# Softmax denominators of an attention layer: when they are summed, and in groups of how many heads

## The chip, the cores and the metric

The kernel runs on one core of a Trainium2 chip. Its engines work at the same time and wait for each other by semaphores: TensorE (PE in the profile) multiplies matrices, VectorE (DVE) adds and multiplies tiles, ScalarE (ACT) evaluates functions and copies, GpSimd (POOL) does elementwise work and issues DMAs, SyncE (SP) issues DMAs. The metric is the device time of one execution in microseconds (us), the median of several.

## The reference

The input x has 4 images (batches) of 1024 channels and 32 x 32 places, so 1024 tokens each. All is float32. Layer 0 is attention with 16 heads of 64, layer 1 a bottleneck of convolutions with batch norms.

```python
x = hidden_states.reshape(B, C, N).transpose(0, 2, 1); residual = x
qkv = (x @ w_qkv.T + b_qkv).reshape(B, N, 3, nh, hd)
q, k = rmsnorm(rope(q)), rmsnorm(rope(k))            # norm over all heads of a token
attn = softmax(einsum('bqhd,bkhd->bhqk', q, k) * hd ** -0.5)
ctx = einsum('bhqk,bkhd->bqhd', attn, v)
x = rmsnorm(ctx @ w_proj.T) + residual               # layer 0
y = relu(bn(conv1x1(x))); y = relu(bn(conv3x3(y))); y = bn(conv1x1(y))
out = relu(x + softplus(residual_scale) * y)         # layer 1
```

The kernel leaves the bias of v out of v and adds it to the context, since the weights of a softmax sum to one.

## The kernel before

The batches run one after the other. Each has four projections (q, k, v, and y after the attention) and the attention itself. The projections of all batches but parts of the first use two nested levels of a scheme that needs seven block products instead of eight; each of its 49 quarter products is four matmuls of 256 columns. The weights' sums for it are prepared once, for a large part on DVE during the attention of batch 0 ("made", lines L397 to L400 and L414 to L417), written back to memory by POOL (L402, L419) and loaded from there by SP (L388, L411) into a ring of eight slots.

Attention of a batch goes over two halves of the queries (`c`, 512 queries each) and in each over eight head pairs (`hp`). A pair has eight steps `t`, one for each 128 keys: PE computes the scores of both heads (L786) into one of three score banks (`sc`, two PSUM banks each), ACT takes the exponential (L793) into `p`, and DVE adds `p` to the pair's denominators (L804, L806: 128 keys x 2 heads x 512 queries). Then PE multiplies the exponentials with v (L815); ACT copies the context (L821). The context comes in two parts. In batch 0 the second is copied by ACT (L824) and added by a DMA of POOL (L825), in the others DVE adds it (L850).

What is left of a denominator is a sum over the 128 partitions, and PE does it, with a matrix of ones. Two pairs, so four heads, form a group (`sums_of_four`, L868: four matmuls of 128x32 into one bank `dn`). The step is kept in the list `late` and runs in the next pair after step 1; for the last group of a batch it runs at once at the end of the attention (`last_inverses`). In the first half of the queries of batches 1 to 3 the denominators are first folded: DMAs of POOL (`halve`, L878 to L881) add the lower and the upper 64 partitions, so that one group of four matmuls (`sum_of_eight`, L887) serves eight heads. It runs at the end of the second pair after its last one.

After a group the reciprocals follow. ACT copies `dn` out (L915, L889, L928), SP writes it to memory and reads it back with few values a partition (L903, L907), DVE takes the reciprocal (L919, L894), SP writes it (L920, L895) and reads it broadcast over the partitions (L937). This second part, `invert`, lies in the list `half_done`; one entry is taken at the end of a pair. The tiles so loaded go to the list `ready`, and at the end of every second pair `mean_of_v` multiplies the contexts by them on DVE (L769) and adds the bias of v on POOL (L770). For the last group the reciprocal is taken of the whole tile (L929), with POOL's DMAs, and the products come in the projection.

Order: PE, POOL, DVE and ACT execute in the order in which the program text issues (`manual_schedule`); only SP's instructions are ordered by the framework. In the projections steps can be put off with `after(n, step)`, n in units of four matmuls of 512 columns or eight of 256 (about 3.43 us); `product_done` runs those that are due. In the attention, weight preparation (`extra`) is spread over the pairs by a count of `slots`, and `load_parts` loads at step 3 so that at most two sets are held.

PSUM is divided anew for each stage:

```python
"proj": [("o1", [P, CH], 4), ("o2", [P, CH], 4)],
"att": [("sc", [P, 2, CH], 3), ("cx", [P, 2, CH], 1)],
```

Of the kernel before, what the change touches and what calls it, by code (L numbers as in the profile page):

```python
# [18 lines left out]
P = 128  # L19
# [66 lines left out]
def program(ctx, tc, x, wblk, w2, w3, vecs, cos, sin, out, bad):  # L86
# [76 lines left out]
    with tc.tile_pool(name=f"st{u}", bufs=2) as st, ExitStack() as s:  # L163
# [95 lines left out]
        def after(n, step):  # L259
            later.append((pace["at"] + n, step))  # L260
# [505 lines left out]
        def mean_of_v(q_all, c, hp, w, engine=nc.gpsimd):  # L766

            cx = q_all[:, hp, half[c]]
            nc.vector.tensor_tensor(cx, cx, w, ALU.mult)  # L769
            engine.tensor_scalar(cx, cx, col("bv", hp), None, ALU.add)  # L770

        def attention(b, c, q_all, k_all, v, probs_, late, ready, extra, slow, steps_in_all, load_parts, fold, then):


            at = half[c]
            sums_, contexts = [], []
            for hp in range(NHP):
                n = f"{b}_{c}_{hp}"
                rows = shifts(q_all, k_all, n, hp, c) if bad is None else None
                probs = []  # L780
                for t in range(N // P):
                    p = probs_[:, t]
                    sc = bank("sc", f"sc_{n}_{t}")
                    for keys in (low, high):
                        for j, d in enumerate((low, high)):
                            nc.tensor.matmul(  # L786
                                sc[keys, j], k_all[d, hp, t * P + keys.start : t * P + keys.stop], q_all[d, hp, at],
                                start=True, stop=bad is not None,
                            )
                    if bad is None:  # L790
                        for j in range(2):
                            nc.tensor.matmul(sc[:, j], ones[0:1, :], rows[j], start=False, stop=True)
                    nc.scalar.activation(p, sc, AF.Exp)  # L793
                    if t == 1:
                        if late:
                            late.pop(0)()
                        if fold and hp % 2 == 0:
                            d_ = fold[hp // 4][:, hp % 4 // 2 * 2 : hp % 4 // 2 * 2 + 2, :]
                        else:
                            d_ = acc.tile([P, 2, CH], F32, tag="tot", name=f"den_{n}")  # L800
                    if t == 3:
                        load_parts()
                    if t == 1:
                        nc.vector.tensor_tensor(d_, probs[0], p, ALU.add)  # L804
                    elif t > 1:
                        nc.vector.tensor_tensor(d_, d_, p, ALU.add)  # L806
                    probs.append(p)
                if (c, hp) == (NCH - 1, NHP - 1):
                    then()
                o = bank("cx", f"cx_{n}")  # L810
                for t in range(N // P):
                    for j in range(2):
                        h0 = (2 * hp + j) * HD
                        for i, keys in enumerate((low, high)):
                            nc.tensor.matmul(  # L815
                                o[j * HD : (j + 1) * HD, i], v[keys, t, h0 : h0 + HD], probs[t][keys, j],
                                start=(t == 0), stop=(t == N // P - 1),
                            )
# [30 lines left out]
                if contexts:  # L849
                    nc.vector.tensor_tensor(contexts[0][0], *contexts.pop(0), ALU.add)  # L850
                if eights and eights[0][0] <= c * NHP + hp:
                    eights.pop(0)[1]()
                if hp % 2 == 0 or fold:
                    continue
                if (c, hp) == (NCH - 1, NHP - 1):
                    last_inverses(b, c, hp, n, sums_of_four(n, sums_), ready)
                else:
                    late.append(lambda n=n, hp=hp, ds=sums_: inverses(b, c, hp, n, sums_of_four(n, ds), ready))
                sums_ = []

        def sums_of_four(n, sums_):
            if n == f"0_{NCH - 1}_{NHP - 1}":
                bank("sc", f"skip_{n}")
            dn = bank("sc", f"dn_{n}")[:, 0]
            for i, d_ in enumerate(sums_):
                for j in range(2):
                    q = slice((2 * i + j) * QH, (2 * i + j + 1) * QH)
                    nc.tensor.matmul(dn[q, :], ones[:, :QH], d_[:, j], start=True, stop=True)  # L868
            return dn

        half_done, eights = [], []
        low, high = slice(0, P // 2), slice(P // 2, P)

        def halve(hp, d_, home):
# [5 lines left out]
                nc.gpsimd.dma_start(home[high], d_[high])  # L880
                nc.gpsimd.dma_start(home[high], d_[low], accum_op=ALU.add)  # L881

        def sum_of_eight(b, n, hp, home, ready):

            dn = bank("sc", f"dn_{n}")[:, 0]
            for i in range(4):
                nc.tensor.matmul(dn[i * QH : (i + 1) * QH, :], halves, home[:, i, :], start=True, stop=True)  # L887
            r = temp(f"rec_{n}")
            nc.scalar.copy(r, dn)  # L889
            k = 2 * b * NCH * NHP + 2 * (hp - 3)  # L890
            few, rows = to_few(n, k, 8, r[:: QH // 2, :])

            def invert():
                nc.vector.reciprocal(few, few)  # L894
                nc.sync.dma_start(rows, few)  # L895
                for i in range(2):
                    at = k + 4 * i
                    spread(0, hp - 2 + 2 * i, n + f"_{i}", ready, [dens[at : at + 2, :], dens[at + 2 : at + 4, :]])
# [11 lines left out]
        def inverses(b, c, hp, n, dn, ready):  # L910


            r = temp(f"rec_{n}")
            k = 2 * ((b * NCH + c) * NHP + hp - 1)
            nc.scalar.copy(r, dn)  # L915
            few, rows = to_few(n, k, 4, r[::QH, :])

            def invert():
                nc.vector.reciprocal(few, few)  # L919
                nc.sync.dma_start(rows, few)  # L920
                spread(c, hp, n, ready, [dens[k + j : k + j + 3 : 2, :] for j in range(2)])
# [293 lines left out]
        for b in range(B):  # L1215
# [60 lines left out]
            slow = [lambda: None] * 3 + [lambda f=f: add_residual(f) for f in range(NT)] if b > 0 else []  # L1276
            probs_ = xp.tile([P, N // P, 2, CH], F32, tag="x", name=f"p_{b}")
            fold = [None, None]
            if b > 0:
# [10 lines left out]
            for c in range(NCH):  # L1290
                if (b, c) == (B - 1, NCH - 1):
                    extra = filters()
                attention(
                    b, c, q_all, k_all, v, probs_, late, ready, extra, slow, steps_in_all, load_parts, fold[c], then
                )
            psum_for("proj")
            room = v_room(f"to_{b}")
# [419 lines left out]
```

## Time and profile before

| what | us |
|---|---|
| median of 3 runs (lowest, highest) | 2649.51 (2647.75, 2649.77) |
| the profiled execution | 2648.69 |
| its span in the profile | 2646.9 |
| PE busy | 2627.9 (99%) |
| DVE busy | 2140.0 (81%) |
| ACT busy | 1122.9 (42%) |
| POOL busy | 470.8 (18%) |
| dn groups of four heads (L868), of eight (L887) | 20 and 6, 8 matmul records each |

The profile shows one execution. A line of its groups gives the program's line, the engine, the operation, out<-in with shapes, the count, then busy time and mean ns, then idle time before and what ended it. A float32 matmul appears as two records. A line of the timeline gives start, length, engine, line and count, and in brackets the engine's idle time before it. A line of the chain gives start, length, what. A line of the waits gives who waited for whom: us in total, times, the longest.

### The profile page before, as it was taken

What the parts mean: (1) busy time and instruction counts of PE and PEld (TensorE: products, weight loads), DVE (VectorE), ACT (ScalarE), POOL (GpSimd) and SP (SyncE); (2) the same over time, 40 slices, a digit from 0 to 9 for tenths busy, and PEclk for the clock granted to TensorE, in tenths of its full rate; (3) what the DMA queues carried; (4) which work ended last, traced back from release to release, by engine and by line L of the source; (5) the groups of instructions that cost most, each with busy time, mean ns of one, the idle gap of its engine ahead of it and who ended that gap; (6) DMA issues with size and microseconds to landing.
All of it is one profiled execution on the core that took longest, in us unless ns stands there. A gap on an engine that the chain in (4) does not pass through costs nothing.

```text
span 2646.9 us, 40534 instructions
## 1 busy us (share of the span) xinstructions
PE 2627.9 (99%) x15452; PEld 1629.4 (62%) x15452; DVE 2140.0 (81%) x2566; ACT 1122.9 (42%) x1576; POOL 470.8 (18%) x592
## 2 busy tenths in 40 slices
PE   9999999999999999999999999999999999999997
PEld 4448433488888333688886333888884335846843
DVE  5567899998887977887878767987988779877977
ACT  2222566523442655433343655233425654312266
POOL 2542244301101221100111222000111221010000
PEclk9999999999999999999999999999999999999999
DMA  8887788777667452456665541665774442683165
GB/s 286 290 255 203 219 253 243 239 224 238 183 182 213 83 103 50 132 179 223 191 191 155 97 85 27 215 206 176 193 213 90 84 105 82 206 279 104 64 235 211
DMA packets 252938, 463.66 MB, mean 175 GB/s; under 512 B 32192, under 2 KB 125168, under 8 KB 252736
## 3 DMA queue, kind: packets, MB, share of 16 engines
q1 hardware_dynamic: 196816, 287.80, 34.3%
q0 software_dynamic: 47856, 156.40, 23.8%
q10 hardware_dynamic: 8064, 16.78, 1.8%
q8 instruction: 125, 2.05, 0.3%
q14 instruction: 77, 0.63, 0.1%
HBM read 329.53 MB, written 97.01 MB: 161 GB/s over the span
## 4 chain that ended last, share of the span: by engine, by line
PE 67%; DVE 1%; ACT 0%; DMA 0%; issue 0%; ACTq 0%
PE sc L786 13%; PE cx L815 12%; PE p_y L490 10%; PE p_v L485 8%; PE p_q L490 6%; PE p_k L490 6%; PE c L1618 3%; PE c2x L1478 2%; PE c2y L1478 2%; PE c L1020 2%; PE c L979 1%; PE c1s L1020 1%; PE dn L868 0%; PE c1a L1020 0%; DMA cosT<-in_cos_dram 0%; ACT h L1602 0%
## 5 line engine op out<-in xcount | busy, mean ns | idle before, releaser
L793 ACT ACTIVATE p<-sc 128x1024 f32<-128x1024 f32 x512 | 478.2, 1049 | 17.7 <-PE sc L786 17.5
L786 PE MATMUL sc<-q,k 64*64 64x512 f32 x4096 | 456.7, 591 | 0.1
L806 DVE TENSOR_TENSOR den<-den,p 128x1024 f32<-128x1024 f32 x312 | 385.5, 1236 | 37.6 <-ACT p L793 5.1
L815 PE MATMUL cx<-p,to 64*64 64x512 f32 x3072 | 338.2, 589 | 0.0
L786 PEld LDWEIGHTS sc<-q,k 64*64 64x64 f32 x4096 | 149.2, 132 | 294.8 <-ACT p L793 151.4
L815 PEld LDWEIGHTS cx<-p,to 64*64 64x64 f32 x3072 | 117.5, 133 | 212.1 <-issue 210.7
L485 PE MATMUL p_v<-w_v,x 128*128 128x256 f32 x928 | 210.0, 379 | 0.8 <-DVE x L456 0.7
L490 PE MATMUL p_y<-q,w_y 128*128 128x256 f32 x928 | 209.8, 379 | 0.7 <-issue 0.7
L490 PEld LDWEIGHTS p_y<-q,w_y 128*128 128x128 f32 x928 | 176.0, 190 | 27.9 <-issue 4.1
L485 PEld LDWEIGHTS p_v<-w_v,x 128*128 128x128 f32 x928 | 176.1, 190 | 26.1 <-DVE x L456 1.3
L821 ACT COPY q<-cx 128x512 f32<-128x512 f32 x64 | 37.5, 585 | 348.0 <-PE cx L815 348.0
L770 POOL TENSOR_SCALAR q<-q,vec 128x512 f32<-128x512 f32 x56 | 108.7, 1966 | 290.3 <-DVE q L769 290.3
L490 PE MATMUL p_q<-to,w_q 128*128 128x256 f32 x672 | 152.2, 379 | 0.0
L490 PE MATMUL p_k<-to,w_k 128*128 128x256 f32 x672 | 152.2, 379 | 0.0
L490 PEld LDWEIGHTS p_k<-to,w_k 128*128 128x128 f32 x672 | 127.4, 190 | 18.4 <-issue 1.2
L490 PEld LDWEIGHTS p_q<-to,w_q 128*128 128x128 f32 x672 | 127.4, 190 | 18.4 <-issue 1.2
L815 PE MATMUL cx<-p,rq 64*64 64x512 f32 x1024 | 112.7, 589 | 0.0
L1618 PE MATMUL c<-h,w 128*128 128x512 f32 x256 | 110.3, 592 | 0.5 <-ACT h L1520 0.5
L804 DVE TENSOR_TENSOR den<-p 128x1024 f32<-128x1024 f32 x52 | 63.5, 1222 | 42.6 <-ACT p L793 42.6
L806 DVE TENSOR_TENSOR den_T<-den_T,p 128x1024 f32<-128x1024 f32 x72 | 88.2, 1225 | 7.5
L485 PE MATMUL p_v<-w_v,t 128*128 128x256 f32 x384 | 90.1, 379 | 0.0
L490 PE MATMUL p_y<-to,w_y 128*128 128x256 f32 x384 | 90.1, 379 | 0.0
(505 smaller groups left out, 4308.5 us busy)
## 6 DMA issues: line engine op xcount, KB each, us to landing
w_v<-wd2f SPq DMA_DIRECT2D x112, 256.0 KB, 3.0
w_y<-wd2f SPq DMA_DIRECT2D x112, 256.0 KB, 3.0
w_q<-wd2f SPq DMA_DIRECT2D x84, 256.0 KB, 2.7
w_k<-wd2f SPq DMA_DIRECT2D x84, 256.0 KB, 2.8
wd2f<-w_pre POOLq DMA_DIRECT2D x68, 256.0 KB, 4.5
q<-qs POOLq DMA_DIRECT2D x64, 256.0 KB, 5.4
k<-ks POOLq DMA_DIRECT2D x64, 256.0 KB, 4.6
x1df<-y POOLq DMA_DIRECT2D x32, 512.0 KB, 5.5
```

The costliest lines, as they stand in the source:

```text
L485: nc.tensor.matmul(o[:, q].rearrange("p (g f) -> p g f", g=2), r[:, i, q * P : (q + 1) * P], wt[:, :, i, :], skip_group_check=True, **at,)
L490: nc.tensor.matmul(o[:, q], wt[:, q, i, :], r[:, i, :], skip_group_check=True, **at)
L770: engine.tensor_scalar(cx, cx, col("bv", hp), None, ALU.add)
L786: nc.tensor.matmul(sc[keys, j], k_all[d, hp, t * P + keys.start : t * P + keys.stop], q_all[d, hp, at], start=True, stop=bad is not None,)
L793: nc.scalar.activation(p, sc, AF.Exp)
L804: nc.vector.tensor_tensor(d_, probs[0], p, ALU.add)
L806: nc.vector.tensor_tensor(d_, d_, p, ALU.add)
L815: nc.tensor.matmul(o[j * HD : (j + 1) * HD, i], v[keys, t, h0 : h0 + HD], probs[t][keys, j], start=(t == 0), stop=(t == N // P - 1),)
L821: nc.scalar.copy(cx, o[:, 0])
L1020: nc.tensor.matmul(o, wt[:, i, :], rows(i), start=first and i == 0, stop=last and i == NH - 1, skip_group_check=True,)
L1478: nc.tensor.matmul(o[:, r * TR * TC : (r + 1) * TR * TC], uw[2 * h + r, j][:, i * PL + f * P : i * PL + (f + 1) * P], vt[b, i][:, 2 * h + ...
L1618: nc.tensor.matmul(os[i], w3t[k][f // NH][:, f % NH, :], h2[b, k][:, half[c]], start=(k == 0), stop=(k == NPT - 1),)
```

## The change

In batch 0 the denominators get a place of their own: two tiles (`own`) used in turn by the groups, instead of the two of the pool `acc`. The sum over partitions runs after step 3 of the next pair instead of step 1 (in the last but one pair still after step 1). `invert` runs after step 2 of the following pair rather than at the end of the pair before it, with exceptions near the end. Batch 0's multiplications by the reciprocals come at the end of even pairs, and the bias of v is added by ACT (`mean_and_bias`, after steps 5 and 6) instead of POOL; in the very last pair by DVE.

In batches 1 and 2 the first four pairs of the second half of queries are folded too, into the tile of the first half's first group. Their group of eight runs one pair after its last pair (in the first half still two pairs after), and its products come at the pair before the last.

The last group of batches 0, 1 and 2 runs half a product into the projection of y, into a bank of the pool `o2`. Weight preparation is spread over 14 instead of 15 pairs.

```diff
-        def attention(b, c, q_all, k_all, v, probs_, late, ready, extra, slow, steps_in_all, load_parts, fold, then):
+        def attention(b, c, q_all, k_all, v, probs_, late, ready, extra, slow, steps_in_all, load_parts, fold, then, own):
...
+            fold_two = 0 < b < B - 1
+            homes = fold
             for hp in range(NHP):
+                fold = homes if homes and hp // 4 < len(homes) else None
...
                     nc.scalar.activation(p, sc, AF.Exp)
+                    if t == (3 if b == 0 and (c, hp) != (NCH - 1, NHP - 2) else 1) and late:
+                        late.pop(0)()
+                    if t in (5, 6) and biases:
+                        biases.pop(0)()
+                    if b == 0 and t == 2 and half_done and half_done[0][0] < c * NHP + hp:
+                        half_done.pop(0)[1]()
                     if t == 1:
-                        if late:
-                            late.pop(0)()
-                        if fold and hp % 2 == 0:
+                        if b == 0:
+                            d_ = own[hp % 4 // 2][:, hp % 2 * 2 : hp % 2 * 2 + 2, :]
+                        elif fold and hp % 2 == 0:
...
-                sums_.append(d_)
-                if hp % 2 == 1:
+                if contexts and b == 0:
+                    add_context(*contexts.pop(0))
+                if not fold:
+                    sums_.append(d_)
+                if hp % 2 == min(b, 1) or c == NCH - 1 and (hp == NHP - 1 or fold_two and hp == NHP - 2):
                     for r in ready:
-                        mean_of_v(q_all, *r)
+                        if b > 0:
+                            mean_of_v(q_all, *r)
+                        elif (c, hp) == (NCH - 1, NHP - 1):
+                            mean_of_v(q_all, *r, nc.vector)
+                        else:
+                            mean_and_bias(q_all, *r)
                     ready.clear()
                 if fold:
                     halve(hp, d_, fold[hp // 4][:, hp % 4 // 2 * 2 : hp % 4 // 2 * 2 + 2, :])
                     if hp % 4 == 3:
-                        eights.append((hp + 2, lambda n=n, hp=hp: sum_of_eight(b, n, hp, fold[hp // 4], ready)))
+                        home = fold[hp // 4]
+                        eights.append(
+                            (c * NHP + hp + 2 - c, lambda n=n, hp=hp, home=home: sum_of_eight(b, c, n, hp, home, ready))
+                        )
...
-                slots = NCH * NHP - 1
+                slots = NCH * NHP - 2
...
                 if (c, hp) == (NCH - 1, NHP - 1):
-                    last_inverses(b, c, hp, n, sums_of_four(n, sums_), ready)
+
+                    def last(ds=sums_):
+                        last_inverses(b, c, hp, n, sums_of_four(n, ds), ready)
+
+                    if b + 1 < B:
+                        after(0.5, last)
+                    else:
+                        last()
...
         def sums_of_four(n, sums_):
-            if n == f"0_{NCH - 1}_{NHP - 1}":
-                bank("sc", f"skip_{n}")
-            dn = bank("sc", f"dn_{n}")[:, 0]
+            dn = bank("o2", f"dn_{n}") if "o2" in psum else bank("sc", f"dn_{n}")[:, 0]
...
+        def add_context(cx, other):
+            nc.vector.tensor_tensor(cx, cx, other, ALU.add)
+
+        def mean_and_bias(q_all, c, hp, w):
+            cx = q_all[:, hp, half[c]]
+            nc.vector.tensor_tensor(cx, cx, w, ALU.mult)
+            biases.append(lambda: nc.scalar.activation(cx, cx, AF.Identity, bias=col("bv", hp)))
...
-            half_done.append((hp + 3, invert))
+            half_done.append((c * NHP + hp + 3 - c, invert))
...
-            half_done.append((0, invert))
+            half_done.append((c * NHP + hp + (1.5 if hp < NHP - 3 or c < NCH - 1 else 1) if b == 0 else 0, invert))
...
+            if b == 0:
+                own = [tp.tile([P, NH, CH], F32, tag=t, name=f"den_{b}_{t}") for t in ("T0", "T2")]
             if b > 0:
 
-                fold[0] = [tp.tile([P, NH, CH], F32, tag=t, name=f"den_{b}_{t}") for t in ("T0", "T2")]
+                fold[0] = homes = [tp.tile([P, NH, CH], F32, tag=t, name=f"den_{b}_{t}") for t in ("T0", "T2")]
+                fold[1] = homes[:1] if b + 1 < B else None
```

More of the change, by code (lines that the diff above doesn't have):

```diff
@@ L848, in attention @@
                     extra.pop(0)()
-                if contexts:
-                    nc.vector.tensor_tensor(contexts[0][0], *contexts.pop(0), ALU.add)
+                if contexts and b > 0:
+                    add_context(*contexts.pop(0))
                 if eights and eights[0][0] <= c * NHP + hp:
@@ L869, in sums_of_four @@
             return dn
-        half_done, eights = [], []
+        half_done, eights, biases = [], [], []
+        def add_context(cx, other):
[4 more added lines that the diff above has]
+            biases.append(lambda: nc.scalar.activation(cx, cx, AF.Identity, bias=col("bv", hp)))
         low, high = slice(0, P // 2), slice(P // 2, P)
@@ L881, in halve, with sum_of_eight @@
                 nc.gpsimd.dma_start(home[high], d_[low], accum_op=ALU.add)
-        def sum_of_eight(b, n, hp, home, ready):
+        def sum_of_eight(b, c, n, hp, home, ready):
             dn = bank("sc", f"dn_{n}")[:, 0]
@@ L889, in sum_of_eight @@
             nc.scalar.copy(r, dn)
-            k = 2 * b * NCH * NHP + 2 * (hp - 3)
+            k = 2 * ((b * NCH + c) * NHP + hp - 3)
             few, rows = to_few(n, k, 8, r[:: QH // 2, :])
@@ L897, in invert @@
                     at = k + 4 * i
-                    spread(0, hp - 2 + 2 * i, n + f"_{i}", ready, [dens[at : at + 2, :], dens[at + 2 : at + 4, :]])
-            half_done.append((hp + 3, invert))
+                    spread(c, hp - 2 + 2 * i, n + f"_{i}", ready, [dens[at : at + 2, :], dens[at + 2 : at + 4, :]])
+            half_done.append((c * NHP + hp + 3 - c, invert))
         def to_few(n, k, rows_, r):
@@ L1278, in program @@
             fold = [None, None]
+            own = None
+            if b == 0:
+                own = [tp.tile([P, NH, CH], F32, tag=t, name=f"den_{b}_{t}") for t in ("T0", "T2")]
             if b > 0:
-                fold[0] = [tp.tile([P, NH, CH], F32, tag=t, name=f"den_{b}_{t}") for t in ("T0", "T2")]
+                fold[0] = homes = [tp.tile([P, NH, CH], F32, tag=t, name=f"den_{b}_{t}") for t in ("T0", "T2")]
+                fold[1] = homes[:1] if b + 1 < B else None
             tc_, two = [], []
@@ L1293, in program @@
                 attention(
-                    b, c, q_all, k_all, v, probs_, late, ready, extra, slow, steps_in_all, load_parts, fold[c], then
+                    b, c, q_all, k_all, v, probs_, late, ready, extra, slow, steps_in_all, load_parts, fold[c], then, own
                 )
```

## Prediction

> **What bounds the kernel now.** I read the busy line first, then the waits of TensorE, then its timeline around the softmax denominators.
>
> ```profile
> PE 2627.9 (99%) x15452; PEld 1629.4 (62%) x15452; DVE 2140.0 (81%) x2566; ACT 1122.9 (42%) x1576; POOL 470.8 (18%) x592
> PE dn L868 <- DVE den L806: 0.9, 1, 0.9
> PE p_y L490 <- issue: 0.7, 1, 0.7
> ```
>
> TensorE (PE) is busy for 2627.9 of 2646.9 us. So only two things can be won: PE instructions that disappear, and the few places where PE stands. The two waits shown are both at the end of batch 0's attention. A third place is no wait in the list; it shows as a stretched group in PE's timeline of batch 0:
>
> ```profile
> 343.77 1.07 PE L868 MATMUL dn<-den,ones 128*32 128x512 f32 x8
> ...
> 372.41 2.21 PE L868 MATMUL dn<-den,ones 128*32 128x512 f32 x8
> ...
> 508.03 7.05 PE L815 MATMUL cx<-p,rq 64*64 64x512 f32 x64
> 515.00 1.05 PE L868 MATMUL dn<-den,ones 128*32 128x512 f32 x4
> 516.98 1.05 PE L868 MATMUL dn<-den,ones 128*32 128x512 f32 x4 [0.92 <-DVE den L806]
> 518.76 3.69 PE L490 MATMUL p_y<-q,w_y 128*128 128x256 f32 x16 [0.73 <-issue]
> ```
>
> The dn group at 372.41 takes 2.21 us where the one before takes 1.07: half of it runs, then it waits. The last group waits for VectorE (DVE), and the first projection matmul starts when ScalarE (ACT) has copied dn (518.08 to 518.66). DVE's timeline says why: it has no gap before those two points, and its last additions end late.
>
> ```profile
> 365.64 7.87 DVE L806 TENSOR_TENSOR den<-den,p 128x1024 f32<-128x1024 f32 x6
> ...
> 402.54 1.60 DVE L400 TENSOR_TENSOR w_pre<-w_pre,w_pre 128x512 f32<-128x512 f32 x1
> ...
> 509.05 7.87 DVE L806 TENSOR_TENSOR den<-den,p 128x1024 f32<-128x1024 f32 x6
> ```
>
> They end at 373.4 and 516.8, after PE asked at 372.4 and 515. In batches 1 and 2 nothing waits; there only the number of dn groups counts. The chain of waits gives the price of one, of four heads inside a head pair and of eight between two:
>
> ```profile
> 1511.10 1.00 PE dn L887 x8
> 1512.10 7.03 PE sc L786 x64
> ...
> 1596.97 1.72 PE sc L786 x16
> 1598.69 1.00 PE dn L868 x8
> 1599.68 5.31 PE sc L786 x48
> ```
>
> Scores of a pair alone take 6.87 us. 1.72 + 1.00 + 5.31 = 8.03 and 1.00 + 7.03 = 8.03, so either kind of group costs 1.16 us: 1.00 of its own and 0.16 around it.
>
> **What the Trainium skill says.** "TensorEngine Tiling (Array Packing)", Key Properties: a change of tiling mode drains the array. The dn tiles are 128x32 between 64x64 ones; the 0.16 us agrees. "GPSIMD Engine Reference", Specifications: GpSimd (POOL) shares its SBUF interfaces with VectorE and they contend when a VectorE instruction has two SBUF inputs. The trace agrees: the 1.60 us above, 0.69 for its neighbours, lies under POOL's bias additions (402.6 to 406.1). "ScalarE: Activation LUTs", Table sets: identity is in every set. So a bias by Identity between exponentials should load no table; the trace shows copies between exponentials without a load, but no Identity there. "DMA: Bandwidth & Descriptors", Anatomy of one DMA: about 2.0 us fixed plus bytes/436e3, an estimate of 2.6 us for 256 KB; the trace has 2.9 for the copy of a fold and 3.5 for its accumulation, and I use these.
>
> **The change, part by part.**
>
> 1. *Batch 0, later groups.* dn moves from step 1 to step 3 of the next pair's eight, 2 x 0.86 = 1.72 us later. The group at 372.4 waited until 373.4, so its 1.14 us (2.21 − 1.07) go. The group itself keeps its 1.16. Score banks: at step 3 dn takes the bank of step 1, whose exponential (0.93 us pitch, from 1.2 us after the pair's start) ends at about 3.1 us, and PE comes at 3.44. No new wait.
>
> 2. *Batch 0's biases* leave POOL (L770, 14 there, 1.97 us mean over the kernel). Twelve go to ACT as Identity, price by the same shape:
>
> ```profile
> L636 ACT ACTIVATE k<-k,vec 128x512 f32<-128x512 f32 x48 | 34.5, 719 | 2.6 <-DVE k L530 2.6
> ```
>
> Two of 0.72 us in every second pair, after the exponentials of steps 5 and 6: the last exponential then ends at 1.2 + 8 x 0.93 + 1.4 = 10.1 us, and PE needs it at 6.87 + 6.0 = 12.9. Hidden, with 2.8 us spare. Two go to DVE (0.49 each). DVE gains what contention cost: the excess over 0.69 of the stretched additions between 346 and 492 sums to about 5.5 us.
>
> 3. *Weight preparation* on DVE is spread over 14 pairs instead of 15: 21 sets of 2.73 us, so 3.0 instead of 2.8 in two pairs, and none is left after pair 6 of the second half. In the profile two sets (502.2 to 507.7) stand ahead of the last pair's additions. Without them these follow the exponentials and end some 10 us after that pair's start, so before PE is done with it (13.7). Per two pairs DVE then has 2 x 9.1 additions + 8.2 preparation + 1.4 reciprocal and multiplications = 27.8 us, against PE's 2 x 13.73 + 1.16 = 28.6. Its cover is 0.8 us per two pairs.
>
> 4. *The reciprocals of batch 0* move from the pair's end to step 2 of the next one. On DVE this is 0.16 us. On SP the write-back, its landing (2.0) and two broadcasts come some 6 us later, and the weight loads queued behind them with them. Those loads wait for free slots anyway (53.4 us of SP's waits in this batch are on written-back weights), and POOL writes them back about 3.5 us sooner without its biases. I price it at 0; bounds −0.5 to +1.5 us of PE time.
>
> 5. *Last group of batches 0 to 2* goes inside the projections, after the first product. Batch 0: from the end of the last pair (514.90) to the first product are 3.86 us; what stays is a group of 1.0 + 0.1. Gain 2.76 us. Batches 1 and 2: 1.06 us before, 1.1 expected after: 0, bounds −0.1 to +0.2 together. The long reciprocal (3.34) and what follows come 0.7 us later; of the sums behind it, those that PE needs first (L287) end at 1674.6 in batch 2 and PE reads them at 1677.7, so 3.1 us cover it.
>
> 6. *Batches 1 and 2, second half:* two groups of four become one of eight: 2 x 1.16 = 2.32 us less on PE. POOL gets six fold DMAs per batch, SP one round trip fewer.
>
> 7. *A new wait.* This group of eight runs one pair after its last head pair; in the first half it is two. POOL does four biases ahead of the last fold. The same sequence stands in the first half of batch 2, for the pair that ended at 1539.7:
>
> ```profile
> 1538.87 8.03 POOL L770 TENSOR_SCALAR q<-q,vec 128x512 f32<-128x512 f32 x4 [12.54 <-DVE q L769]
> 1546.86 0.58 POOL L880 DMA_DIRECT2D den_T<-den  x1
> 1550.09 0.83 POOL L881 DMA_DIRECT2D den_T<-den  x1 [2.66 <-DMA den_T<-den]
> ```
>
> 1550.09 + 3.5 to 3.8 = 1553.6 to 1553.9, 13.9 to 14.2 us after the pair's end. PE asks after 13.73, and behind dn stands the whole next pair. Half of dn's operands are older, which hides up to 0.5; in the second half the biases took 8.36. I take +0.6 us per batch, 1.2 in all; bounds 0 and 2.0.
>
> **Sum:** −1.14 − 2.76 − 2.32 + 1.2 + 0.2 (small delays of parts 4 and 5) = −4.8 us. The profiled execution took 2648.69 us (span 2646.9 and 1.8 around it): 2643.9. It lies 0.8 below the median of the runs shown, 2649.51, so this is 5.6 us (0.21%) below the median. A measurement of this kernel can tell about 0.2%, 5.3 us, from no change; the forecast is just past that.
>
> **Rivals.** *B, the gain is eaten.* The fold arrives late at its upper bound (+2.0 instead of 1.2) and batch 0 still waits for DVE: the first half's third set of weights is asked for a pair earlier, and SP stands there for 28.6 us on slots, so dn at step 3 can wait again, 1 to 2 us. Then 2 to 3 us remain, 2646. For it: DVE's cover is 0.8 us. Against: the waits of DVE on DMA in this batch sum to only 4.9 us now.
>
> *C, slower: DVE becomes batch 0's bound.* Each late load stalls DVE before its additions; what exceeds the cover of 0.8 us per two pairs accumulates over seven groups, and dn waits. To lose 5.3 us in spite of a gain of 4.8, 10.1 us must come up: 0.8 + 10.1/7 = 2.2 us of DMA wait per two pairs, against 4.9/7 = 0.7 now. At 3 us it would be 7 x 2.2 = 15.4 less 4.8: 2659. For it: part 4 delays loads, and the later DVE is, the later SP. Against: slots, not SP, set the loads.
>
> *D, tables:* if Identity were not in the set of the exponential, two biases with an exponential between them would bring four loads (1.28 us each in the trace), 5.1 us, 2.3 over part 2's spare, six times: +14 us. The page excludes it; I leave it 0.01.
>
> **How the numbers follow.** Forecast 0.58, at 2642 to 2644.2; B 0.30, 2644.2 to 2648; C and D 0.12, above 2654.8. The low end takes parts 1, 5, 6 whole, no new wait, and 1 us of spread: 2648.7 − 6.2 − 1 = 2641.5. The high end holds B and the beginning of C: 2651.
>
> **What would show it.** In the profile after: no stretched dn in batch 0 and none waiting for den; projections start within 0.2 us of the last pair; 16 groups of four heads and 8 of eight, where 20 and 6 were before; Identity activations of 0.7 us among batch 0's exponentials without table loads; no POOL bias there. Part 7 is wrong if dn of the second half does not wait for the accumulation. A DVE in batch 0 that waits more than 2 us per two pairs on weights, with dn behind it, would make the whole prediction wrong.

## The result, and the profile after

The changed kernel takes 2646.06 us (median of 22 runs, 2645.12 to 2648.66), the kernel before in the same job 2649.47 (22 runs, 2647.66 to 2652.57). The ratio is 0.9987, with a 95% interval from 0.9982 to 0.9993: a gain of 3.4 us, 0.13%, which lies within the 0.2% that the prediction called no change. The point was 2643.9, 2.2 us too low. The range from 2641.5 to 2651.0 holds the result, the interval called likeliest, 2642 to 2644.2, does not: the range is right because it was wide enough for rival B. By its size the result is rival B, "the gain is eaten" (2646). What ate it is only in part what B named.

The profiled execution took 2645.64 us, its span is 2643.8 (before 2648.69 and 2646.9). In the changed program L893 is the group of four heads (L868 before), L921 the group of eight (L887), L815 the additions to the denominators (L806), L824 the context (L815), L899 the addition of the context's two parts (L850). The busy line and TensorE's waits on what the attention or the projections give, the p_v and p_y lines of the changed kernel:

```profile
PE 2624.5 (99%) x15436; PEld 1628.9 (62%) x15436; DVE 2136.3 (81%) x2566; ACT 1128.4 (43%) x1586; POOL 451.9 (17%) x590
...
PE p_v L485 <- DVE x L456: 1.5, 2, 0.9
...
PE p_y L490 <- issue: 0.8, 2, 0.4
```

PE has 16 records fewer: two dn groups of eight records each. The two waits of before at the end of batch 0 are gone. In their place there are two of p_y at the ends of batches 1 and 2, and p_v waits twice where it waited once. PE's timeline of the changed kernel in batch 0, at the second and third group and at the end:

```profile
345.18 1.07 PE L893 MATMUL dn<-den_T,ones 128*32 128x512 f32 x8
...
373.81 1.07 PE L893 MATMUL dn<-den_T,ones 128*32 128x512 f32 x8
...
506.57 7.05 PE L824 MATMUL cx<-p,rq 64*64 64x512 f32 x64
513.55 1.99 PE L490 MATMUL p_y<-q,w_y 128*128 128x256 f32 x8
515.47 1.06 PE L893 MATMUL dn<-den_T,ones 128*32 128x512 f32 x8
516.47 1.99 PE L490 MATMUL p_y<-q,w_y 128*128 128x256 f32 x8
```

No group is stretched, and the projection starts at 513.55, when the context ends. The same view of the changed kernel at the group of eight in the second half of batch 1, and at the end of that batch:

```profile
1037.89 1.86 PE L921 MATMUL dn<-den_T,halves 128*32 128x512 f32 x8
...
1084.12 1.06 PE L893 MATMUL dn<-den,ones 128*32 128x512 f32 x8
1085.59 1.97 PE L490 MATMUL p_y<-q,w_y 128*128 128x256 f32 x8 [0.41 <-issue]
```

The group of eight takes 1.86 instead of 1.06: it waits 0.80 in its middle. Then the second product of the projection (the next eight p_y records) waits 0.41. In batch 2 it is 1.35 for the group (0.29) and 0.40 for the product.

A ledger of all stages comes from two marks in each batch in PE's timeline: the first matmul of the scores, and the first p_y matmul with y as its input, which follows the second product of the projection. The table gives how much longer (+) or shorter (−) each stretch is than in the profile of the kernel before, in us. Each column is one execution; the forecast's +0.2 for small delays stands in no row.

| stretch | predicted | after | e1 | e2 | e9 | e3 | e4 | e5 |
|---|---|---|---|---|---|---|---|---|
| attention of batch 0 | −3.9 | −4.05 | −3.60 | −2.69 | −3.22 | −1.99 | −2.59 | −3.36 |
| projections, to batch 1 | 0 | +0.16 | +0.24 | +0.58 | +0.05 | −0.02 | −0.08 | −0.08 |
| attention of batch 1 | −0.56 | +0.28 | 0.00 | +0.18 | +0.54 | −0.52 | −0.34 | −0.96 |
| projections, to batch 2 | 0 | +0.88 | −0.05 | +0.84 | +0.94 | +0.47 | +0.75 | +0.15 |
| attention of batch 2 | −0.56 | −0.23 | 0.00 | −0.12 | +0.21 | −0.50 | −0.68 | −0.95 |
| projections, to batch 3 | 0 | +0.35 | 0.00 | +0.43 | −0.01 | +0.21 | +0.53 | −0.01 |
| attention of batch 3 | 0 | −0.52 | −0.15 | −0.52 | −0.50 | −0.51 | −0.51 | −0.50 |

The attention of batch 3 is not changed. Most of its −0.5 belongs to the profile of before: DVE stands for 0.46 us there between two of its own additions (at 2205.49), and the last group of batch 3 is stretched to 1.49 us, against 1.14 in the changed kernel. In e1 DVE stands 0.46 in the same stretch of batch 3, the group takes 1.50, and the gain is missing.

### The profile page after: what moved, and what is told of

The parts are those of the page before. It is cut to its first block, busy times and chain, and to the rows that moved or that the text cites. A ratio compares the mean times of both kernels' runs of the same rounds, so it can differ in the third digit from the quotient of the medians.

```text
span 2643.8 us, 40486 instructions
## 1 busy us (share of the span) xinstructions
PE 2624.5 (99%) x15436; PEld 1628.9 (62%) x15436; DVE 2136.3 (81%) x2566; ACT 1128.4 (43%) x1586; POOL 451.9 (17%) x590
## 5 line engine op out<-in xcount | busy, mean ns | idle before, releaser
L824 PE MATMUL cx<-p,to 64*64 64x512 f32 x3072 | 338.2, 589 | 0.0
L815 DVE TENSOR_TENSOR den<-den,p 128x1024 f32<-128x1024 f32 x192 | 237.9, 1239 | 21.9 <-ACT p L796 2.2
L815 DVE TENSOR_TENSOR den_T<-den_T,p 128x1024 f32<-128x1024 f32 x192 | 236.3, 1231 | 20.4 <-DVE den_T L815 1.4
L824 PEld LDWEIGHTS cx<-p,to 64*64 64x64 f32 x3072 | 117.5, 133 | 212.1 <-issue 211.0
L770 POOL TENSOR_SCALAR q<-q,vec 128x512 f32<-128x512 f32 x42 | 80.5, 1926 | 215.6 <-DVE q L769 215.6
L824 PE MATMUL cx<-p,rq 64*64 64x512 f32 x1024 | 112.7, 589 | 0.0
L732 POOL DMA_DIRECT2D k<-ks x64 | 57.6, 1087 | 180.2 <-ACT p L796 71.3
```

The source lines that it names most:

```text
L732: nc.gpsimd.dma_start(dst[i::2, f, :], other[1 - i :: 2, :], accum_op=ALU.add)
L824: nc.tensor.matmul(o[j * HD : (j + 1) * HD, i], v[keys, t, h0 : h0 + HD], probs[t][keys, j], start=(t == 0), stop=(t == N // P - 1),)
```

## Experiments

Four kernels (e1, e2, e5, e9) share one chip and 47 runs of the kernel before (2649.86), four more (e3, e4, e6, e7) another (23 runs, 2649.51), and the last four (e8, e10, e12, e13) a third (41 runs, 2648.65). Each is compared with the kernel before of its own job. The diffs are against the changed kernel.

**e1: batch 0 alone.** No second fold, and the last group goes into the projection in batch 0 only.

```diff
-            fold_two = 0 < b < B - 1
+            fold_two = False
-                    if b + 1 < B:
+                    if b == 0:
                         after(0.5, last)
-                fold[1] = homes[:1] if b + 1 < B else None
```

> The kernel after with batches 1 and 2 as before (no second fold, their last group at the end of the attention); batch 0 as changed. Theory: the whole gain is batch 0's (4.0 us up to the second product of its y projection), and batches 1 and 2 gave nothing, so this kernel is as fast as the kernel after within 0.5 us: 2645.5, ratio to before 0.9985. Rival, the forecast's own sum: batches 1 and 2 are worth 1.1 us, so this is 1 us slower than after, 2647. On the table waits in the v projections (0.85, 0.67 and a stretch of 0.35 after, one of 0.68 before): if the change in batches 1 and 2 makes them, batches 2 and 3 show none here; if they are scatter or come from batch 0, they show.

Measured: 2647.19, ratio 0.9990 (0.9982 to 0.9998), 2.7 us less. The whole measurable gain is batch 0's. The ledger shows nothing in the stages of batches 1 and 2.

**e9: no second fold**, the last groups still in the projections.

```diff
-            fold_two = 0 < b < B - 1
+            fold_two = False
-                fold[1] = homes[:1] if b + 1 < B else None
```

> The kernel after without the second fold of batches 1 and 2: four groups of four in their second half, the last one still inside the projection. Theory: two groups more cost 2.32 us, the two waits of dn for the fold (1.09) are gone: 1.2 us slower than after, 2647.3, and batches 1 and 2 are then slower than before by their second products' waits. Rival: the fold's DMAs cost PE more than their wait (banks, slower DMAs elsewhere), then this is as fast as after.

Measured: 2647.47, 0.9990 (0.9981 to 0.9998). Against e1 it adds only the last groups of batches 1 and 2, and these stages get 0.54 and 0.21 longer. So moving the group in is not free: 0.31 of batch 1 is a wait of the second product, and about 0.2 in each batch goes without a wait (from the last matmul of the context to the first product with y it takes 5.27 us in batch 2, where it took 5.07 before).

**e2: the last groups of batches 1 and 2 stay at the end**, with the second fold.

```diff
-                    if b + 1 < B:
+                    if b == 0:
                         after(0.5, last)
```

> The kernel after, but the last group of batches 1 and 2 runs at the end of the attention as before; the second fold stays. Theory: inside the projection the group shifts the banks of o2, and the second product waits 0.41 and 0.40 us until VectorE has read the last context; here both waits are gone and the group costs 1.06, so 0.8 to 1.0 us faster than after: 2645.1. Rival: those waits are the price of any group of 128x32 tiles between projections, and appear here in another place: same as after, 2646.

Measured: 2646.73, 0.9989 (0.9982 to 0.9996), no better than the change. The price came up in another place. PE's timeline of e2 at the end of batch 1, then ACT's:

```profile
1083.37 1.06 PE L893 MATMUL dn<-den,ones 128*32 128x512 f32 x8
1085.18 3.69 PE L490 MATMUL p_y<-q,w_y 128*128 128x256 f32 x16 [0.75 <-issue]
```

```profile
1084.50 0.58 ACT L962 COPY rec<-dn 128x512 f32<-128x512 f32 x1 [0.41 <-PE dn L893]
```

Now the first product waits, 0.75 us in both batches (batch 1: −1.16 for the group, +0.55 for the fold, +0.75 here, so +0.14 of the measured +0.18), and starts 0.10 us after ACT has copied dn. Before the change batch 0 had the same picture (copy to 518.66, product at 518.76). One group fewer moves the turn of the score banks by one, and a reading is that dn then lies where the first product's bank comes to lie. This is read from the times; it was not tried alone, and one thing speaks against it: in the kernel before, dn of batch 0 is the 137th request for a score bank and dn of batch 1 the 134th, the same place if three banks take turns, yet only batch 0's product waited. Without the fold (e1) the same order costs nothing. With the fold but without the deferral, these stages gain nothing.

**e3: the fold ahead of the multiplications by the reciprocals and of POOL's biases** (first diff). **e4: the context's addition ahead of these multiplications**, on DVE, in the last pair (second diff). **e5: both.**

```diff
+                if fold:
+                    halve(hp, d_, fold[hp // 4][:, hp % 4 // 2 * 2 : hp % 4 // 2 * 2 + 2, :])
...
                 if hp % 2 == min(b, 1) or c == NCH - 1 and (hp == NHP - 1 or fold_two and hp == NHP - 2):
                     for r in ready:
...
-                if fold:
-                    halve(hp, d_, fold[hp // 4][:, hp % 4 // 2 * 2 : hp % 4 // 2 * 2 + 2, :])
...
```

```diff
-                if contexts and b == 0:
+                if contexts and (b == 0 or b + 1 < B and (c, hp) == (NCH - 1, NHP - 1)):
                     add_context(*contexts.pop(0))
```

> The kernel after, POOL issues the fold DMAs of a pair ahead of its biases, nothing else. Theory: the last fold of the second half lands about 8 us earlier, and the groups of eight in the second half of batches 1 and 2 take 1.06 us instead of 1.86 and 1.35. The second products still wait 0.4 us. Rival: the fold waits for VectorE's additions or for the memory, not for the biases, then the groups stay at 1.3 to 1.9.

> The kernel after, in the last pair of batches 1 and 2 VectorE adds the context ahead of the two multiplications, nothing else. Theory: the second product of the y projection waits for VectorE's reading of the last context bank (done 0.1 us before it starts), so it starts 0.4 us earlier with no wait. Rival: it waits for ScalarE's copy of dn or for the array's change of mode, then the 0.4 us stay.

> The kernel after with two orders changed: POOL issues the fold DMAs of a pair ahead of the biases of the same pair, and in the last pair of batches 1 and 2 VectorE adds the context ahead of the multiplications. Theory: the dn waits of the second half (0.80 and 0.29) and the waits of the second product (0.41 and 0.40) go, 1.9 us: 2644.2, and the gain of the two groups saved then shows. Rival: something else is late by then (the biases end later, the products after them), and less than 1 us comes: 2645.3.

e3 took 2645.79 and e4 2645.76 (one run each); what they tell is in their profiles. POOL's timeline for the fold of batch 1's second half, first the changed kernel, then e3:

```profile
1023.31 8.11 POOL L770 TENSOR_SCALAR q<-q,vec 128x512 f32<-128x512 f32 x4 [12.21 <-DVE q L769]
1031.37 0.60 POOL L914 DMA_DIRECT2D den_T<-den  x1
1035.14 0.82 POOL L915 DMA_DIRECT2D den_T<-den  x1 [3.17 <-DMA den_T<-den]
```

```profile
1024.69 0.55 POOL L914 DMA_DIRECT2D den_T<-den  x1 [11.81 <-DVE den L815]
1027.88 0.80 POOL L915 DMA_DIRECT2D den_T<-den  x1 [2.64 <-DMA den_T<-den]
1028.45 6.73 POOL L770 TENSOR_SCALAR q<-q,vec 128x512 f32<-128x512 f32 x4
```

Four biases stood ahead of the fold. With the fold first, the accumulation is issued 11.8 us ahead of the group (it starts at 1039.69 in e3) instead of 2.75, the group of eight takes 1.06 in both batches, and the biases themselves run in 6.73 instead of 8.11. The second product still waits, 0.40 and 0.41. In e4 it is the other way round: no wait of the second product, and the group of eight at 1.69 and 1.34. So these are two separate causes. DVE's timeline at the end of batch 1, the changed kernel and then e5, shows the second one:

```profile
1083.61 1.28 DVE L769 TENSOR_TENSOR q<-q,inv 128x512 f32<-128x512 f32 x2
1084.81 0.68 DVE L899 TENSOR_TENSOR q<-q,cx 128x512 f32<-128x512 f32 x1
```

```profile
1083.58 0.68 DVE L899 TENSOR_TENSOR q<-q,cx 128x512 f32<-128x512 f32 x1
1084.18 1.29 DVE L769 TENSOR_TENSOR q<-q,inv 128x512 f32<-128x512 f32 x2
```

The second product starts 0.10 us after the addition of the context ends (1085.49) in the changed kernel. In e5 that addition is done 1.2 us earlier. The list of PE's waits in e5:

```profile
PE warm L1241 <- DVE halves L103: 1.1, 1, 1.1
PE p_v L485 <- DVE x L456: 0.6, 1, 0.6
PE c L1656 <- ACT h L1558: 0.5, 1, 0.5
PE pa_k L308 <- DVE w_k_3b L243: 0.3, 1, 0.3
```

No wait of an attention stage is among them. e5 measured 2644.03 (11 runs), 0.9978 (0.9969 to 0.9987), so 5.8 us less than the kernel before, and in the same job 2.7 less than e2, 3.4 less than e9. Against the changed kernel itself the comparison goes through two jobs (ratios 0.9978 and 0.9987, whose intervals overlap by 0.0005), so by the times alone it is likely, and not shown, that it is faster; in the profiles its attentions of batches 1 and 2 are 1.24 and 0.72 us shorter. Each of batches 1 and 2 gains 0.95 in it, where a group of four less is worth 1.16. The missing 0.2 is the cost, seen in e9 too, of a group that stands between two products: here too the way from the context to the first product with y is 5.27 us.

**e6: all groups after step 1.**

```diff
-                    if t == (3 if b == 0 and (c, hp) != (NCH - 1, NHP - 2) else 1) and late:
+                    if t == 1 and late:
```

> The kernel after, with batch 0's groups after step 1 again instead of step 3; its other edits (order of means, biases on ScalarE, 14 pairs of preparation) stay. If the later step is what removed the wait of 1.14 us, a stretched dn group of about 2 us shows again at the third of batch 0, 1 us slower, 2647. If the other edits made VectorE early enough, no group waits and the time stays at 2646.

Measured: 2647.83, 0.9993 (0.9984 to 1.0002); batch 0's attention −1.96. The third group, which waited before the change, does not wait here. The second one does. From the second group to the third it takes 30.19 us instead of 28.63, so 1.56 are lost.

**e7: weight preparation over 15 pairs again.**

```diff
-                slots = NCH * NHP - 2
+                slots = NCH * NHP - 1
```

> The kernel after, with weight preparation spread over 15 pairs again. If the preparation ahead of the last pair's additions made them late, they end about 5 us later here, and the last dn group of batch 0, now 1.9 us into the projection, waits about 0.5 to 1.5 us: 2647. If the move into the projection alone was enough, nothing waits: 2646.

Measured: 2650.33, 1.0002 (0.9993 to 1.0011); batch 0's gain is gone (+0.22). PE's timeline of e7 at the end of batch 0, then DVE's:

```profile
516.40 1.76 PE L893 MATMUL dn<-den_T,ones 128*32 128x512 f32 x8
520.24 3.59 PE L490 MATMUL p_y<-q,w_y 128*128 128x256 f32 x8 [2.08 <-DVE q L899]
```

```profile
507.26 0.69 DVE L400 TENSOR_TENSOR w_pre<-w_pre,w_pre 128x512 f32<-128x512 f32 x1
507.87 1.22 DVE L813 TENSOR_TENSOR den_T<-p 128x1024 f32<-128x1024 f32 x1
...
519.51 0.68 DVE L899 TENSOR_TENSOR q<-q,cx 128x512 f32<-128x512 f32 x1
```

The preparation (L400) stands ahead of the last pair's additions, and all that DVE does after them is late as well. 0.70 go in the group (1.76 for 1.06), 2.08 ahead of the second product, 1.60 inside it (3.59 for 1.99): 4.4 us, three times the most that was expected. The second group (346.11) has its normal 1.07.

**e8: batch 0's biases on POOL again.**

```diff
-                            mean_and_bias(q_all, *r)
+                            mean_of_v(q_all, *r)
```

> The kernel after with batch 0's biases on POOL again, all else as after. If the contention of POOL's biases with VectorE (additions of 0.69 us stretched to 1.0 to 1.6) is what the move to ScalarE removes, the stretched additions come back, VectorE is some 5 us later over batch 0 and later groups wait: 1 to 2 us slower, 2647.5. If the other edits give enough room, no dn group waits but those of after: 2646.

Measured: 2648.49 against 2648.65, 0.9997 (0.9989 to 1.0006); batch 0 −0.11. POOL's timeline of e8, DVE's beside it, and the group of PE that follows:

```profile
392.25 4.27 POOL L770 TENSOR_SCALAR q<-q,vec 128x512 f32<-128x512 f32 x2 [2.38 <-DVE q L769]
```

```profile
395.12 1.06 DVE L400 TENSOR_TENSOR w_pre<-w_pre,w_pre 128x512 f32<-128x512 f32 x1
```

```profile
404.65 1.75 PE L893 MATMUL dn<-den_T,ones 128*32 128x512 f32 x8
```

Under POOL's two biases DVE's operation takes 1.06 instead of 0.69; its additions end at 405.3, and the group that began at 404.65 waits. This group and the one at 489.52, where DVE is stretched by as much and also stands 0.46, lose 0.68 and 1.43 by their distances; neither waits with the biases on ACT. The second group (346.41) loses 0.98, but its additions run under no bias of POOL, and this lies within what it loses with the biases on ACT (0 to 1.4, see below).

**e10, e12, e13: two attempts to win more.** e10 puts off the tables of sines in the projections (first diff). e12 is e5 with one set of weights fewer at the second pair of batch 0 (second diff). e13 is e12 with e10.

```diff
-                    pace["tables"] = pace["at"] + (4.3 if b == 1 else 3.7)
+                    pace["tables"] = pace["at"] + 5.5
```

```diff
-                for _ in range(len(extra) - -(-steps_in_all * max(slots - 1 - c * NHP - hp, 0) // slots) if steps_in_all else 0):
+                for _ in range(len(extra) - ((c, hp) == (0, 1)) - -(-steps_in_all * max(slots - 1 - c * NHP - hp, 0) // slots) if steps_in_all else 0):
```

> The kernel after, with the multiplications of the rotary tables put off to 5.5 instead of 3.7 or 4.3 products after the tables' loads are issued. Theory: in the v projections VectorE waits 4.4 us for the sine table and stands 0.5 to 1.7 us more for the cosine, and the sums that PE needs next (x, L456) stand behind them; put off, they go ahead, and the waits of 0.85, 0.67 and the stretch of 0.35 are gone: 1.9 us or a little more with the restarts, 2644.1. Rival: the turns that follow come too late for the attention and PE waits there: 2646 or more.

> The kernel with both orders changed (folds ahead of biases, context ahead of multiplications), and in the second pair of batch 0 one set of weights is made instead of two. Theory: VectorE waits there 3.6 to 4.7 us for the third set, and so the second dn group of batch 0 waits 0.4 to 0.8 us in most profiles; with one set that wait is gone, VectorE has no wait over 2 us in the first five pairs, and no group of batch 0 waits: 0.5 to 1 us faster than the kernel with both orders alone, 2643.3. Rival: the set is then late one pair later and the third group waits: no gain, 2644.

> All four: folds ahead of biases, context ahead of multiplications, one set in the second pair, tables put off. Theory: the parts add up, 2644.0 less 0.7 less what is left of the table waits there (0.6 in batch 1): 2642.6, ratio to before 0.9972. Rival: put-off tables cost in the attention of batches 1 to 3, and this is no faster than 2643.3.

e10 measured 2646.05, 0.9991 (0.9982 to 0.9999), e12 2648.87, 0.9999 (0.9990 to 1.0007), e13 2648.16, 0.9997 (0.9989 to 1.0005). None won. In e10 the waits of p_v stay, 0.76 and 0.58. In e12 the second group no longer waits, and the third does, as PE's timeline shows:

```profile
376.16 1.05 PE L893 MATMUL dn<-den_T,ones 128*32 128x512 f32 x4
380.80 1.92 PE L893 MATMUL dn<-den_T,ones 128*32 128x512 f32 x4 [3.59 <-DVE den_T L815]
```

That execution took 2651.5, 2.6 above e12's median, so the wait may usually be shorter; in e13's profile it is 1.92. The set that was left out comes later, DVE waits 7.36 us for its load ahead of the third group's additions, and the wait is moved, not removed.

## Why the forecast came out this way

**Batch 0 (parts 1, 3 and 5), −3.9: near the profile of the changed kernel (−4.05), which is in part luck, and 0.9 too much as a mean.** Eight profiles have the changed program for batch 0 (after, e1, e2, e3, e4, e5, e9, e10, the last with −2.39). Their gains go from 1.99 to 4.05, and their mean is 3.0. Two terms are the same in all eight: the third group no longer waits (1.14, as forecast), and from the last matmul of the context to the first product with y it takes 5.27 us instead of 7.81. That is 2.54 for part 5, where 2.76 were forecast; the group between two products costs 0.2 here as well. Together 3.68. The way from the first scores to the first group adds some scatter: without the 1.72 of the later step it is 0.38 shorter than before in the changed kernel's profile, up to 0.43 longer in others, and 0.13 longer in the mean. What varies most is the second group, as rival B had it: with 14 pairs a third set of weights falls into the second pair, and DVE waits for its load. DVE's timeline of the changed kernel and of e4, and e4's group:

```profile
320.96 0.69 DVE L414 TENSOR_TENSOR w_blk<-w_blk,w_blk 128x512 f32<-128x512 f32 x1 [3.60 <-DMA w_blk<-in_wblk_dram]
```

```profile
322.62 0.69 DVE L414 TENSOR_TENSOR w_blk<-w_blk,w_blk 128x512 f32<-128x512 f32 x1 [4.67 <-DMA w_blk<-in_wblk_dram]
```

```profile
345.81 1.78 PE L893 MATMUL dn<-den_T,ones 128*32 128x512 f32 x8
```

The wait lies between 3.6 and 4.8 us in these profiles. The second group's loss, by its distance to the third, is 0 in two of them, 0.3 to 0.9 in five and 1.4 in e3. The mean is 0.6, where B had 1 to 2, and 3.68 less 0.6 and 0.1 is the mean gain of 3.0. With 15 pairs (e7) there is no such wait and no loss. So B's mechanism is there, at a smaller price. The prediction named a DVE that waits more than 2 us per two pairs on weights, with dn behind it, as the sign that all of it is wrong. That sign is there in six of the eight profiles, and it cost 0.3 to 1.4 us: it was drawn too sharply.

- *Part 1* (1.14): the wait at the third group is gone, but e6 shows that it is gone at step 1 too. Step 3 pays at the second group: with a wait for the third set of 3.6 to 3.85 us this group loses 0 to 0.7 in four of the eight profiles, and 1.56 in e6 with 3.79. e6 gains 1.0 less than the mean of the eight, about the predicted size for another group than predicted.
- *Part 2*, hidden: right. Twelve Identity activations of 0.79 us (forecast 0.72) stand between exponentials, and the count of table loads is unchanged (five at L702, four at the exponentials). Their line in the groups of the changed kernel, with mean and idle time:

```profile
L904 ACT ACTIVATE q<-q,vec 128x512 f32<-128x512 f32 x12 | 9.4, 786 | 0.0
```

This agrees with the Trainium skill, "ScalarE: Activation LUTs", Table sets. e8 shows that the part, which the sum has at nothing of its own, is needed: without it (−0.11) the batch is 2.9 us slower than the mean of the eight, 2.1 of them at two groups that wait in none of the eight. The contention that the same skill describes in "GPSIMD Engine Reference", Specifications, is seen there as 1.06 for 0.69.
- *Part 3*: right in its mechanism and larger than thought, since e7 loses 4.4 us at the end of the batch. Part 5's gain in batch 0 exists only with it.
- *Part 4* at nothing: no run contradicts it, and none tests it alone.

**Batches 1 and 2 (parts 5, 6, 7): forecast −1.1 together, measured +0.05. The term that failed is part 5.** The groups (part 6) are 16 and 8, as said, and worth 1.16 each. The fold's wait (part 7), 1.2 forecast, is 0.80 + 0.29 = 1.09, by the cause named, the biases ahead of it (e3). Part 5 was put at 0 for these batches, with bounds up to +0.2. It costs 0.41 + 0.40 for the second product's wait, plus about 0.24 in each batch without a wait. The sum comes to −2.32 + 1.09 + 0.81 + 0.48 = +0.06. I had costed the deferred reciprocal and its readers, but not the addition of the context, which DVE does behind two multiplications and which the second product now waits for (e4).

Two things make this wait. The first is that the need itself is new. PE's timeline of e1 at the end of batch 1, where the group runs ahead of the first product as before, and DVE's:

```profile
1084.43 3.72 PE L490 MATMUL p_y<-q,w_y 128*128 128x256 f32 x16
```

```profile
1085.95 0.68 DVE L899 TENSOR_TENSOR q<-q,cx 128x512 f32<-128x512 f32 x1
```

The second product follows the first without a stop: it starts at 1086.27, while DVE's addition runs until 1086.63. It reads the same data in both orders; what the change alters for it is its PSUM bank. The second product writes the first bank that the projection asks of the pool `o2`, and with the deferral dn takes this one, so that the second product gets the next. The likely reading is that DVE still has to read the last context out of that bank; no trace shows where the banks lie.

The second is that DVE is late. PE leaves the context 1.1 us after the end of DVE's additions in the changed kernel, instead of 1.55. DVE's timeline before and in the changed kernel, then POOL's in the changed kernel:

```profile
1075.63 1.23 DVE L804 TENSOR_TENSOR den<-p 128x1024 f32<-128x1024 f32 x1 [1.53 <-ACT p L793]
1076.96 7.88 DVE L806 TENSOR_TENSOR den<-den,p 128x1024 f32<-128x1024 f32 x6
```

```profile
1071.43 1.38 DVE L813 TENSOR_TENSOR den<-p 128x1024 f32<-128x1024 f32 x1 [1.53 <-ACT p L796]
1072.92 8.17 DVE L815 TENSOR_TENSOR den<-den,p 128x1024 f32<-128x1024 f32 x6
```

```profile
1067.15 7.09 POOL L770 TENSOR_SCALAR q<-q,vec 128x512 f32<-128x512 f32 x4 [31.19 <-DVE q L769]
```

The first two additions of the last pair take 1.38 and 1.53 instead of 1.23 each, which is the 0.45, and both start under the four biases that the second fold brings to this place; the later ones take 1.23 again. e2, with the second fold, has the same 1.38 and 1.53. e9 has no second fold, and its additions are not stretched: in batch 2 the second product waits only 0.03 there, since the addition ends just in time, and in batch 1, where DVE stands for 0.46 between two additions, it waits 0.31. So the deferral left no room behind this addition, and the fold's biases took more than there was. e5 makes the room again by the order on DVE.

**What no part had:** p_v waits for x in the projections of batch 2 (0.67), loses 0.35 in a stretched group in batch 3, and waits 0.17 more in batch 1. DVE there stands for the table of sines, 4.79 us instead of 4.39 in batch 2, and makes the sums of x (L456) after it. DVE's timeline of the changed kernel, then PE's:

```profile
1387.74 1.23 DVE L720 TENSOR_TENSOR sinT<-sinT,sqk 128x1024 f32<-128x1024 f32 x1 [4.79 <-DMA sinT<-in_sin_dram]
...
1391.95 0.69 DVE L456 TENSOR_TENSOR x<-t,x 128x512 f32<-128x512 f32 x1
```

```profile
1392.69 5.45 PE L485 MATMUL p_v<-w_v,x 128*128 128x256 f32 x24 [0.67 <-DVE x L456]
```

e1 has no such wait in batches 2 and 3, e5 and e9 none in batch 3, and e8, whose projections there are the changed kernel's, none in batch 2 or 3; so it comes and goes between executions, and these profiles don't tell whether the change makes it likelier. e10 missed, and DVE's wait there is still 4.70. Why the table lands later is open. These waits are 1.2 us of the 1.7 by which the span's gain (3.1) falls short of the forecast's 4.8. The failed term of part 5 is 1.3 more; 0.5 of batch 3 and some tenths elsewhere go the other way.

## What to carry to other kernels

When a step is moved into the next stage, list what the waiting engine does *after* it, and ask for each such operation not only what it reads but which buffer it will now be given and who reads that buffer last. Compare the end of that reader in the old trace with the time at which the buffer will be asked for. Ask too under which operations the work of the new step will run: the 0.45 us that POOL's biases took from DVE became a wait of TensorE, because nothing was left to cover it. Put the operation with a reader on the critical engine ahead of those without one; reordering two pairs of steps (e5) turned a fold that gained nothing into one that gains 0.95 us a batch. With an engine that is almost full, such as DVE in batch 0, parts that look separate stand and fall together: taking back one of them (e7, e8) cost batch 0's whole gain.

## What the hardware showed

One wait on a load differs by 1.2 us between executions whose programs are the same for that stage (3.6 to 4.8 us for the third set of weights), and TensorE's stage by 2.06. A difference of that size between two single profiles says nothing, unless the line where it arises is found.

In every profile DVE stands for 0.46 us one to five times between two of its own operations, where nothing else is seen to hold it. The place differs from kernel to kernel: the last pairs of batch 3 before the change, the last pair of batch 1 in e1 and e9. What causes it is open.

POOL's biases stretch DVE's operations that read two tiles: 0.69 us became 1.06 in e8, and 1.23 became 1.38 and 1.53 at the end of batch 1.

A wait of TensorE for ACT's copy of dn, 0.73 us in batch 0 before the change, appeared in e2 in batches 1 and 2 (0.75). That a turn of the banks moves it there is a reading only.
